# Attention scores from one 128-row matmul on twelve-bit parts in place of four 32-row fp32 tiles

## The chip, the cores and the metric

The kernel runs on one core of a Trainium2 chip. The metric is the device time of one execution in microseconds (us), lower is better; the median of three runs is given. In profiles PE is TensorE, PEld its weight loads, DVE VectorE, ACT ScalarE, POOL GpSimd and SP SyncE, which here only issues DMAs.

## What is computed

The input x has four images of 64 x 64 tokens with 256 channels, all fp32. Two layers follow each other. The first is an attention over the 4096 tokens of an image, with keys f and queries g of 32 channels and values of 128. The second is a triangle attention over the 64 x 64 grid with eight heads, followed by a layer norm, an MLP and another layer norm.

```python
xt = x.reshape(b, hw, c)
f = xt @ Wf + bf
g = xt @ Wg + bg
v = xt @ Wh + bh
s = jnp.einsum('bqd,bkd->bqk', g, f)
beta = jax.nn.softmax(s, axis=-1)
o = jnp.einsum('bqk,bkd->bqd', beta, v)
x = x + (o @ Wo + bo).reshape(b, h, w, c)
...
scores = jnp.einsum('bilhd,bljhd->biljh', q, k) / np.sqrt(d_k)
att = jax.nn.softmax(scores, axis=2)
out = jnp.einsum('biljh,bilhd,bljhd->bijhd', att, v1, v2)
h = _layer_norm(x_in + out.reshape(B, N, N, E) @ Wo, ln_agg_g, ln_agg_b)
return _layer_norm(jax.nn.relu(h @ W1 + b1) @ W2 + b2 + h, ln_out_g, ln_out_b)
```

The change concerns f, g and s.

## The kernel before

`run` goes through the four images ("batches") one after the other. For each there is an attention stage (`layer0`) and then a triangle stage (`first_layer1` for batch 0, `next_layer1` for the others).

**The factors g and f.** `factors` (L236) makes g and f of 512 tokens in one PSUM bank; four blocks of 128 tokens lie on the four groups of 32 partitions. ScalarE adds the biases on the way to a tile `gf` in SBUF (`biased`, L248, instructions of L251). The tile is stored to DRAM, g and f apart, and read back in the layout that the scores need: `spread_g` (L255) puts g of all 4096 tokens on 32 partitions, once for each of four partition groups, as the tile `gT` [128, 4096]; `spread_f` (L261) puts a quarter of f on each group, as `fT` [128, 2, 512]. For batch 0 this is done at the start (`front0`), the stores on ScalarE's queue and the spreads on GpSimd's. For batches 1 to 3 it is done ahead, within batch 0's triangle stage: `Ahead` takes 24 pieces s of 512 tokens each through words of a fixed order, `ORDER0`. Word P transposes the input, C copies it, v and u make the values, g makes the factors, a adds the biases and stores (`factored`, L366, whose tile has one buffer); the digit behind the letter names the piece of the period, and "/2" means two periods late. `Ahead.fetch` (L373) reads what batch b + 1 needs while batch b's triangle stage is in its last steps: g at steps 24 to 27, the first half of v at 28, x at 29 and 30, f after the last piece, the rest at the end, all on SP's queue.

**The attention stage.** `layer0` has eight rows of queries (qb, 512 tokens) times eight groups of keys (k, 512 tokens). `scores(g)` (L522) makes the scores of one group as [keys, queries]: four matmuls, each on its own 32 rows of the array, for four blocks of 128 keys. ScalarE takes the exponential of two PSUM banks at a time (L533), `values(g)` multiplies it with v (L544, four matmuls of 128 rows that add up in one bank), and VectorE sums the exponentials for the denominator (L551). The scores of group g + 1 are issued ahead of the values of group g. `parts` puts the work on the previous row of queries behind the groups: at k = 0 the denominator's matmul (L561), reciprocal (L563) and division (L565), at k = 1 the output matmul (L586), then the projections for the second layer.

**The triangle stage.** 32 steps (NSTEP), each with eight products of attention weights and v2 (`product`, L946), two or three of them on GpSimd and the others on VectorE, and the matmuls that sum them (L956). The order of the words in each period is written out by hand in `ORDER0` and `ORDER`. For batches 1 to 3 the layer norms and the MLP of the batch before run among them (`Tokens`), with some small operations and two passes of 128x512 (`finish`, L1182 and L1183) on GpSimd.

**Buffers.** The large tiles share tags of the pool `big`: "v2" has two buffers of 16 KB a partition (v2 of two head pairs, gT, half of v), "qk" one of 16 KB (q and k, half of v), "S" two. `fT` shares the tag "hid".

**A second run.** `run(safe=True)` repeats all with a maximum taken off the scores, only if the recorded denominators leave a range. It isn't executed on these inputs. It uses bf16 copies of g and f (`reduced`, `max_piece`).

Of the kernel before, what the change touches and what calls it, by code (L numbers as in the profile page):

```python
# [11 lines left out]
BF16 = mybir.dt.bfloat16  # L12
AF = mybir.ActivationFunctionType
# [3 lines left out]
P = 128  # L17
# [3 lines left out]
N = 64  # L21
# [33 lines left out]
    t0/1 v2/2 n1/2 R25/2 A25/2 R33/2 sp0/1 T21/2 A32/2 C30/2 R34/2 R36/2 R30/2 A33/2 e00/1 u2/2 e01/1  # L55
    o1/2 R31/2 g2/2 P00/1 c0/1 R37/2 A34/2 A36/2 A30/2 A31/2 A37/2 V0/1 R35/2 C00/1 T30/2 t1/1 R00/1
    p1/2 P01/1 a2/2 C01/1 A35/2 R03/1 T31/2 A00/1 R02/1 g0/1 a0/1 R05/1 R07/1 A05/1 A03/1 v3/2 R06/1
    u3/2 m0/1 S2/1 W2/1 c1/1 v0/1 V1/1 R01/1 A02/1 n0/1 R04/1 A07/1 A01/1 A04/1 R12/1 P11/1 u0/1 P10/1
    A06/1 T00/1 sp1/1 C11/1 T01/1 R13/1 R15/1 R14/1 A13/1 e10/1 e11/1 t2/1 C10/1 R10/1 A12/1 R17/1 V2/1
    A15/1 A14/1 A10/1 R16/1 R11/1 S0 R22/1 W3/1 g3/2 c2/1 W0 A17/1 R27/1 A11/1 v1/1 R20/1 a3/2 u1/1 o0/1  # L60
    p0/1 S1 R21/1 T10/1 P20/1 t3/1 P21/1 A16/1 T11/1 C20/1 A20/1 R23/1 A22/1 R24/1 R26/1
# [4 lines left out]
def attention_then_triangle_kernel(  # L66
# [144 lines left out]
    class Front:  # L211
        def alloc(self, name):
            if name == "g":
                self.gT = big.tile([P, T], F32, tag="v2", name="gT", bufs=2)
            elif name == "f":
                self.fT = work.tile([P, 2, 512], F32, tag="hid", name="fT", bufs=1)
            elif name == "lo":

                lo = big.tile([P, 4096], F32, tag="qk", name="vlo")
                self.fB = lo[:, 2048:2560].bitcast(BF16).rearrange("p (t k) -> p t k", t=2)  # L220
                self.v = [lo[:, 0:2048].rearrange("p (n d) -> p n d", d=P)]
            elif name == "hi":

                hi = big.tile([P, 4096], F32, tag="v2", name="vhi", bufs=2)
                self.gB = hi[:, 2048:4096].bitcast(BF16)
                self.v.append(hi[:, 0:2048].rearrange("p (n d) -> p n d", d=P))
            else:
                if name == "x0":
                    self.yT = []
                self.yT.append(big.tile([P, T], F32, tag="S", name="yT", bufs=2))  # L230

        def reduced(self):
            for q in range(8):
                nc.gpsimd.tensor_copy(self.gB[:, ts(q, 512)], self.gT[:, ts(q, 512)])
            nc.gpsimd.tensor_copy(self.fB, self.fT)
# [11 lines left out]

    def biased(ps, t):  # L248
        ps = ps.rearrange("p (w t) -> p w t", w=4)
        for w, bias in enumerate((bias_g, bias_f)):  # L250
            nc.scalar.activation(t[:, w, 0:P], ps[:, w, :], AF.Identity, bias=bias)  # L251
# [3 lines left out]
    def spread_g(F, r, d, q0=0, q1=8, queue=nc.sync):  # L255
        queue.dma_start(
            out=F.gT[ts(r, CQK), 512 * q0 : 512 * q1].rearrange("c (q t) -> c q t", t=P),
            in_=d[q0:q1].rearrange("q (n c) t -> c (q n) t", n=4),
        )

    def spread_f(F, q, d, queue=nc.sync):  # L261
        queue.dma_start(
            out=F.fT[ts(q % 4, CQK), q // 4, :].rearrange("c (n t) -> c n t", t=P),
            in_=d[q].rearrange("(n c) t -> c n t", n=4),
        )


    def front0(b):
        F = Front()
        for name in ("x0", "x1", "g", "f", "lo", "hi"):  # L270
            F.alloc(name)
        d = {n: dram.tile([8, P, P], F32, tag="ah" + n, name="ah" + n, bufs=NB) for n in ("g", "f")}
# [18 lines left out]
        for q in range(8):  # L291
            ahead = turned(q + 1) if q < 7 else None
            col = ts(q, 512)
            gf = work.tile([P, 2, C], F32, tag="st", name="gf", bufs=3)
            ps = pb("gf")
            factors(ps, [F.yT[cc][:, col] for cc in range(2)])
            biased(ps, gf)
            for w, n in enumerate(("g", "f")):
                nc.scalar.dma_start(out=d[n][q], in_=gf[:, w, 0:P])
            if ahead:  # L300
                taken(*ahead)
            ps = pc("vp")
            for n in range(4):
                for cc in range(2):
                    nc.tensor.matmul(
                        ps[:, ts(n, P)], F.yT[cc][:, ts(q * 4 + n, P)], wh_sb[:, cc, :],
                        start=(cc == 0), stop=(cc == 1),
                    )
            nc.vector.tensor_copy(
                F.v[q // 4][:, q % 4 * 4 : q % 4 * 4 + 4, :], ps.rearrange("p (n d) -> p n d", n=4)  # L310
            )
            if q % 4 == 3:
                for r in range(4):
                    spread_f(F, q - 3 + r, d["f"], nc.gpsimd)
                    spread_g(F, r, d["g"], q - 3, q + 1, nc.gpsimd)
# [4 lines left out]
    class Ahead:  # L320
        def __init__(self):
            shapes = {"x": [C, T], "v": [P, NKC, P], "g": [8, P, P], "f": [8, P, P]}
            self.d = {
                b: {n: dram.tile(sh, F32, tag="ah" + n, name="ah" + n, bufs=NB) for n, sh in shapes.items()}
                for b in range(1, NB)
            }
            self.n = 8 * (NB - 1)
            self.tp, self.xT, self.vp, self.gf = {}, {}, {}, {}
# [37 lines left out]
        def factored(self, s):  # L366
            t = work.tile([P, 2, C], F32, tag="h", name="gf", bufs=1)
            biased(self.gf.pop(s), t)
            for w, n in enumerate(("g", "f")):
                nc.sync.dma_start(out=self.d[1 + s // 8][n][s % 8], in_=t[:, w, 0:P])  # L370


        def fetch(self, F, b, step):  # L373
# [3 lines left out]
            if 24 <= step < 28:  # L377
                spread_g(F, step - 24, d["g"])
            if step == 28:
                F.alloc("lo")  # L380
                nc.sync.dma_start(out=F.v[0], in_=d["v"][:, 0:16, :])
# [5 lines left out]
            if step == 31:  # L387
                F.alloc("f")
                for q in range(8):
                    spread_f(F, q, d["f"])  # L390
            if step == 32:
                F.alloc("hi")
                nc.sync.dma_start(out=F.v[1], in_=d["v"][:, 16:32, :])
                F.alloc("x1")
                nc.sync.dma_start(out=F.yT[1], in_=d["x"][P : 2 * P, :])
# [70 lines left out]
    def layer0(b, F, safe, rest):  # L466
# [4 lines left out]
        if safe:  # L471
            F.reduced()

# [9 lines left out]
        def max_piece(qc, t, mx):  # L483
            rows = slice(32 * (t % 4), 32 * (t % 4) + 32)
            ps = pb("mxp")
            nc.tensor.matmul(ps, F.gB[rows, ts(qc, P)], F.fB[rows, t // 4, :], start=True, stop=True)
            nc.vector.tensor_reduce(mx[:, qc % 4, t : t + 1], ps, AX.X, ALU.max)
# [28 lines left out]
        def scores(g):  # L516
# [3 lines left out]
            for r in range(4):  # L520
                rows = slice(32 * r, 32 * r + 32)
                nc.tensor.matmul(  # L522
                    s_ps[r // 2][:, r % 2, :], fT[rows, tt, ts(n, P)], gT[rows, ts(qb, QB)],
                    start=True, stop=not safe,
                )
            for r in range(4 if safe else 0):
                one = slice(32 * r, 32 * r + 1)
                nc.tensor.matmul(
                    s_ps[r // 2][:, r % 2, :], ones_b[one, :], row[qb][one, :], start=False, stop=True
                )  # L530
# [115 lines left out]
        def proj_qk(qk, st):  # L646
# [14 lines left out]
            nc.scalar.mul(qk[:, 0, 1792:2048], ps[0][:, 0:256], scale1)  # L661
            nc.scalar.copy(qk[64:128, 1, 1536:2048], ps[1][64:128, :])
# [132 lines left out]
    class Layer1:  # L795
# [10 lines left out]
        def fetch_qk(self, pair, first=False):  # L806
            io, rows = self.io, ts(pair, 64)
            qk = self.qk[pair] = big.tile([P, 2, 2048], F32, tag="qk", name="qk")
            n = 56 if first else 64
            for lh in range(2):  # L810
                half, lk = slice(64 * lh, 64 * lh + 64), min(n - 32 * lh, 32) * N
                nc.sync.dma_start(
                    out=qk[half, 0, 0 : 32 * n], in_=io["q"][rows, lh, 0:n, :].rearrange("c i l -> c (i l)")
                )
                nc.sync.dma_start(out=qk[half, 1, 0:lk], in_=io["k"][rows, 2048 * lh : 2048 * lh + lk])


        def fetch_v2(self, pair, part=None):
            if part != 1:
                self.v2[pair] = big.tile([P, 2, D, N], F32, tag="v2", name="v2", bufs=2)  # L820
# [3 lines left out]
        def fetch_rows(self, pair, l0, l1):  # L824
            v2 = self.v2[pair].rearrange("p h d j -> p (h d j)")
            for i2 in range(2):
                nc.sync.dma_start(
                    out=v2[64 * i2 + l0 : 64 * i2 + l1, :],
                    in_=self.io["v2"][l0:l1, ts(pair, 64), :].rearrange("l c j -> l (c j)"),
                )  # L830


        def scores(self, pair, u):
# [3 lines left out]
            q = qk[:, 0, :].rearrange("p (i l) -> p l i", l=32)  # L837
            k = qk[:, 1, :].rearrange("p (l j) -> p l j", j=N)
# [96 lines left out]
        def product(self, step, m):  # L935
# [10 lines left out]
            eng.tensor_tensor(R, src.unsqueeze(1).to_broadcast([P, D, N]), v2[:, h], ALU.mult)  # L946
# [36 lines left out]
    class Tokens:  # L983
# [6 lines left out]
        def load(self, tt, far=False):  # L990
# [4 lines left out]
            if far:  # L995

                tag = ("v2", "S", "qk")[t % 3]
                both = big.tile([P, 2, 2, 256], F32, tag=tag, name="A", bufs=1 if tag == "qk" else 2)
# [328 lines left out]
    def first_layer1(L, ahead, F):  # L1327
# [10 lines left out]
        def front_word(w, s, cc):  # L1338
            if not 0 <= s < ahead.n:
                return  # L1340
            if w == "P":
                ahead.turned(s, cc)
                turned[s] = turned.get(s, 0) + 1
                if turned[s] == 2:
                    ahead.load(s + 1)
                    if s + 1 == ahead.n:
                        ahead.fetch(F, 1, 31)
# [8 lines left out]
            elif w == "a":  # L1356
                ahead.factored(s)

# [21 lines left out]
    def next_layer1(b, L, rest, ahead, F):  # L1380
# [32 lines left out]
        def of_piece(word, q):  # L1413
# [44 lines left out]
            elif word in ("z0", "z1") and second:  # L1458
# [3 lines left out]
                if F is not None and q == n2 - 1 and ("z", 1 - n) in mps[q]:  # L1462
                    ahead.fetch(F, b + 1, 31)
# [87 lines left out]
```

## Times and profile before

| | us |
|---|---|
| median of 3 runs | 3775.97 |
| lowest and highest run | 3773.95 and 3778.14 |
| span of the profiled execution | 3763.4 |
| TensorE busy in it | 3662.3 |
| VectorE busy | 2623.4 |
| ScalarE busy | 1934.5 |
| GpSimd busy | 1728.9 |

The profiled execution is one execution; its span goes from the first to the last instruction. Its time as a run isn't given apart. The runs' median lies 12.6 us above the span, which is taken as what lies around it. The mean granted clock of TensorE is 0.992.

How to read the parts: busy times are unions, so four matmuls that run side by side on four row groups count once. The page lists two matmul instructions for every fp32 matmul of the program (2048 for the 1024 score matmuls). The groups of the score matmuls, of the values' matmuls and of the two kinds of products, from the list of the costliest groups:

```profile
L946 POOL TENSOR_TENSOR Rp<-attP,v 128x2048 f32<-128x2048 f32 x328 | 1490.3, 4573 | 441.3 <-ACT attP L906 387.5
L946 DVE TENSOR_TENSOR R<-att,v 128x2048 f32<-128x2048 f32 x696 | 1548.1, 2273 | 99.1 <-PE acc L956 59.5
...
L544 PE MATMUL o<-e,vlo 128*128 128x512 f32 x1024 | 475.2, 607 | 0.0
...
L522 PE MATMUL s<-gT,fT 32*128 32x512 f32 x2048 | 300.1, 640 | 3.9 <-ACT e L533 3.7
```

Each line gives line, engine, operation, result and operands, shapes and count; then busy us and the mean ns of one; then the engine's idle time just before them and what ended most of it. The attention stages lie at about 41 to 355, 900 to 1320, 1797 to 2215 and 2698 to 3115 us of the span, the triangle stages between and after them.

### The profile page before, as it was taken

The numbers are of one execution on the slowest core, as the hardware profiler recorded it, in microseconds if no ns is written. First come the engines' busy times: TensorE is split into PE (matmuls) and PEld (weight loads), VectorE is DVE, ScalarE is ACT, GpSimd is POOL, SyncE is SP. The second block draws the span as 40 slices with busy tenths as digits, with TensorE's granted clock in tenths as the row PEclk, the third lists the DMA queues.
The fourth block names the chain that finished last, engine by engine and source line by source line (L and its number), as shares of the span: only waits on it lengthen the run. The fifth ranks groups of instructions, "written<-read, shape, count | busy, mean of one in ns | idle before, by whom it ended". The sixth has DMA issues, their size and how long they took to land.

```text
span 3763.4 us, 60343 instructions
## 1 busy us (share of the span) xinstructions
PE 3662.3 (97%) x23626; PEld 1804.7 (48%) x23626; DVE 2623.4 (70%) x2014; ACT 1934.5 (51%) x4257; POOL 1728.9 (46%) x870
## 2 busy tenths in 40 slices
PE   9999999889999999999999999999999999999998
PEld 5444444444444455554344445555344445555477
DVE  3454499897444469999544449999754445999976
ACT  3333466554333367766333346766533335767654
POOL 4000099895000059999100018999600004999920
PEclk9999999999999999999999999999999999999999
DMA  4111466554111254423111153343211116432221
GB/s 119 46 42 42 113 172 152 147 148 143 45 49 47 74 134 95 93 55 93 57 50 45 53 132 89 76 96 71 93 40 45 53 51 153 93 84 61 67 63 55
DMA packets 446215, 313.65 MB, mean 83 GB/s; under 512 B 299680, under 2 KB 408992, under 8 KB 438624
## 3 DMA queue, kind: packets, MB, share of 16 engines
q1 hardware_dynamic: 427472, 295.84, 29.9%
q10 hardware_dynamic: 15184, 8.06, 0.8%
q0 software_dynamic: 3264, 5.78, 0.7%
q8 instruction: 189, 3.10, 0.4%
q14 instruction: 106, 0.87, 0.1%
HBM read 170.07 MB, written 139.46 MB: 82 GB/s over the span
## 4 chain that ended last, share of the span: by engine, by line
PE 83%; POOL 7%; DMA 3%; issue 2%; DVE 2%; ACT 1%; SPq 0%; ACTq 0%; POOLq 0%; DVEq 0%
PE o L544 25%; PE acc L956 17%; PE proj L601 8%; PE s L522 7%; POOL Rp L946 6%; PE mp L1148 5%; PE zp L1168 5%; PE sp L844 3%; PE hp L1015 2%; PE v1p L633 2%; PE y L586 2%; DVE R L946 1%; DMA qk<-k 1%; PE att L898 1%; PE den L561 1%
## 5 line engine op out<-in xcount | busy, mean ns | idle before, releaser
L946 POOL TENSOR_TENSOR Rp<-attP,v 128x2048 f32<-128x2048 f32 x328 | 1490.3, 4573 | 441.3 <-ACT attP L906 387.5
L946 DVE TENSOR_TENSOR R<-att,v 128x2048 f32<-128x2048 f32 x696 | 1548.1, 2273 | 99.1 <-PE acc L956 59.5
L551 DVE TENSOR_TENSOR esum<-esum,e 128x2048 f32<-128x2048 f32 x224 | 512.7, 2289 | 558.5 <-ACT e L533 555.3
L956 PE MATMUL acc<-R,wsel 128*32 128x512 f32 x5568 | 698.7, 599 | 13.4 <-ACT ao L966 7.5
L533 ACT ACTIVATE e<-s 128x1024 f32<-128x1024 f32 x512 | 496.5, 1021 | 404.1 <-PE s L522 394.7
L1076 POOL TENSOR_SCALAR nt<-mv 128x4 f32<-128x4 f32 (+1 forms) x51 | 9.8, 193 | 1286.9 <-DVE mv L1032 1276.0
L544 PE MATMUL o<-e,vlo 128*128 128x512 f32 x1024 | 475.2, 607 | 0.0
L544 PE MATMUL o<-e,vhi 128*128 128x512 f32 x1024 | 472.8, 605 | 0.0
L956 PE MATMUL acc<-Rp,wsel 128*32 128x512 f32 x2624 | 347.7, 602 | 6.2 <-POOL Rp L946 5.4
L966 ACT COPY ao<-acc 128x1024 f32<-128x1024 f32 x256 | 254.6, 1020 | 178.4 <-PE acc L956 165.9
L956 PEld LDWEIGHTS acc<-R,wsel 128*32 128x32 f32 x5568 | 155.4, 109 | 352.3 <-issue 279.0
L544 PEld LDWEIGHTS o<-e,vlo 128*128 128x128 f32 x1024 | 184.6, 190 | 281.8 <-issue 281.8
L544 PEld LDWEIGHTS o<-e,vhi 128*128 128x128 f32 x1024 | 184.3, 189 | 279.7 <-issue 279.7
L522 PE MATMUL s<-gT,fT 32*128 32x512 f32 x2048 | 300.1, 640 | 3.9 <-ACT e L533 3.7
L881 ACT ACTIVATE es<-S,rd 128x64 f32<-128x64 f32 x1024 | 257.8, 336 | 10.2 <-DVE rd L873 8.7
L563 DVE RECIPROCAL rec<-den 128x512 f32<-128x512 f32 x32 | 107.4, 3357 | 217.3 <-PE den L561 217.3
L1148 PE MATMUL mp<-hT,w 128*128 128x256 f32 x1024 | 249.5, 389 | 0.7 <-ACT hT L1120 0.7
L1168 PE MATMUL zp<-w,hid 128*128 128x256 f32 x1024 | 244.9, 384 | 0.8 <-ACT hid L1157 0.8
L1148 PEld LDWEIGHTS mp<-hT,w 128*128 128x128 f32 x1024 | 186.5, 190 | 101.4 <-ACT attP L906 36.0
L1168 PEld LDWEIGHTS zp<-w,hid 128*128 128x128 f32 x1024 | 185.5, 190 | 63.0 <-issue 30.2
L613 ACT COPY st<-proj 128x512 f32<-128x512 f32 x98 | 57.3, 585 | 288.4 <-PE proj L601 160.3
L854 ACT ACTIVATE S<-sp 128x512 f32<-128x512 f32 x128 | 129.6, 1115 | 91.5 <-PE sp L844 91.5
(177 smaller groups left out, 3701.3 us busy)
## 6 DMA issues: line engine op xcount, KB each, us to landing
v<-v2d SPq DMA_DIRECT2D x22, 1024.0 KB
v1c<-v1d SPq DMA_DIRECT2D x128, 128.0 KB
aT<-ao SPq DMA_DIRECT2D x1024, 16.0 KB
A<-aT SPq DMA_DIRECT2D x256, 64.0 KB
out_dram<-z SPq DMA_DIRECT2D x63, 256.0 KB
y<-yT SPq DMA_DIRECT2D x56, 256.0 KB
q<-st SPq DMA_DIRECT2D x56, 256.0 KB
qk<-k SPq DMA_DIRECT2D x28, 512.0 KB
```

Source lines behind the costliest of these rows:

```text
L522: nc.tensor.matmul(s_ps[r // 2][:, r % 2, :], fT[rows, tt, ts(n, P)], gT[rows, ts(qb, QB)], start=True, stop=not safe,)
L533: nc.scalar.activation(e[g][:, 2 * j : 2 * j + 2, :], s_ps[j], AF.Exp)
L544: nc.tensor.matmul(o_ps[qb], F.v[tt][:, r * 4 + n, :], es[:, r, :], start=(k == 0 and r == 0), stop=(k == 7 and r == 3),)
L551: nc.vector.tensor_tensor(esum[qb], esum[qb], es, ALU.add)
L601: nc.tensor.matmul(ps, w[:, cc, rows], y(qb, cc), start=(cc == 0), stop=(cc == 1))
L854: nc.scalar.activation(self.S[pair][:, :, l0 : l0 + 8].rearrange("p i l -> p l i"), sp[:, lh], AF.Copy if self.safe else AF.Exp,)
L881: nc.scalar.mul(e[:, i, :], rows[:, i, :], rec[:, i : i + 1])
L946: eng.tensor_tensor(R, src.unsqueeze(1).to_broadcast([P, D, N]), v2[:, h], ALU.mult)
L956: nc.tensor.matmul(acc[32 * c : 32 * c + 32, n % 2, :], w[:, n, c, 16 * h : 16 * h + 32], R[:, ts(c, 8), :].rearrange("p d j -> p (d j)"), ...
L966: nc.scalar.copy(self.ao[step][:, ts(np, 2)].rearrange("p k d j -> p k (d j)"), self.acc[step][np])
L1148: nc.tensor.matmul(self.mp[:, fc % 2, :], w1_sb[:, cc, ts(fc, P)], self.hT[tt][:, cc, :], start=(cc == 0), stop=(cc == 1),)
L1168: nc.tensor.matmul(zp[:, n, :], self.hid[tt][:, fc, ts(n, P)], w2_sb[:, fc, :], start=(fc == 0), stop=(fc == 3 and tt not in self.hT2),)
```

## The change

`biased` now writes each of g and f twice: as fp32 into t[:, 1] and, as float32r, into t[:, 0]. [...]t[:, 0] is the upper twelve-bit part. `parted` subtracts it from the full value on VectorE, which leaves the lower part. The tile with both parts of both factors (256 KB) is stored in one DMA on SP's queue. The spreads put the parts on the four row groups so that group r holds part r % 2 of g and part r // 2 of f: one matmul over all 128 rows then adds the four products of parts. The tiles gT and fT are float32r in two halves each, and their DMAs are issued on GpSimd's queue. `scores` makes each block of 128 keys with one such matmul.

For the halves, the large buffers are cut in two: "v2" has four of 8 KB and "qk" two; q and k, the halves of v and of v2 become tiles of their own, and v2 is loaded by four DMAs in place of two. For batches 1 to 3, a new word b (`parted`) stands behind each a in `ORDER0`, f is fetched at step 28 and after the last step in place of after the last piece. The bf16 copies and `reduced` go away.

```diff
+PART = mybir.dt.float32r
...
-    t0/1 v2/2 n1/2 R25/2 A25/2 R33/2 sp0/1 T21/2 A32/2 C30/2 R34/2 R36/2 R30/2 A33/2 e00/1 u2/2 e01/1
+    t0/1 v2/2 n1/2 R25/2 A25/2 R33/2 b1/2 sp0/1 T21/2 A32/2 C30/2 R34/2 R36/2 R30/2 A33/2 e00/1 u2/2 e01/1
...
-    p1/2 P01/1 a2/2 C01/1 A35/2 R03/1 T31/2 A00/1 R02/1 g0/1 a0/1 R05/1 R07/1 A05/1 A03/1 v3/2 R06/1
-    u3/2 m0/1 S2/1 W2/1 c1/1 v0/1 V1/1 R01/1 A02/1 n0/1 R04/1 A07/1 A01/1 A04/1 R12/1 P11/1 u0/1 P10/1
+    p1/2 P01/1 a2/2 C01/1 A35/2 R03/1 T31/2 A00/1 R02/1 b2/2 g0/1 a0/1 R05/1 R07/1 A05/1 A03/1 v3/2 R06/1
+    u3/2 m0/1 S2/1 W2/1 c1/1 v0/1 V1/1 R01/1 b0/1 A02/1 n0/1 R04/1 A07/1 A01/1 A04/1 R12/1 P11/1 u0/1 P10/1
...
-    p0/1 S1 R21/1 T10/1 P20/1 t3/1 P21/1 A16/1 T11/1 C20/1 A20/1 R23/1 A22/1 R24/1 R26/1
+    p0/1 S1 R21/1 T10/1 P20/1 t3/1 P21/1 A16/1 T11/1 C20/1 A20/1 R23/1 b3/2 A22/1 R24/1 R26/1
...
-                self.gT = big.tile([P, T], F32, tag="v2", name="gT", bufs=2)
+                self.gT = [big.tile([P, T // 2], PART, tag="v2", name="gT", bufs=4) for _ in range(2)]
...
         for w, bias in enumerate((bias_g, bias_f)):
-            nc.scalar.activation(t[:, w, 0:P], ps[:, w, :], AF.Identity, bias=bias)
+            nc.scalar.activation(t[:, 1, w, :], ps[:, w, :], AF.Identity, bias=bias)
+            nc.scalar.activation(t[:, 0, w, :].bitcast(PART), ps[:, w, :], AF.Identity, bias=bias)
+
+    def parted(t):
+        nc.vector.tensor_tensor(t[:, 1].bitcast(PART), t[:, 1], t[:, 0], ALU.subtract)
...
+    def store_parts(d, q, t, queue):
+        queue.dma_start(out=d[q], in_=t)
...
+    def spread_g(F, r, d, half):
+        nc.gpsimd.dma_start(
+            out=F.gT[half][ts(r, CQK), :].rearrange("c (q t) -> c q t", t=P),
+            in_=d[4 * half : 4 * half + 4, :, r % 2, 0, :].rearrange("q (n c) t -> c (q n) t", n=4),
         )
...
+    def spread_f(F, r, d, half):
+        nc.gpsimd.dma_start(
+            out=F.fT[half][ts(r, CQK), :].rearrange("c (q t) -> c q t", t=P),
+            in_=d[4 * half : 4 * half + 4, :, r // 2, 1, :].rearrange("q (n c) t -> c (q n) t", n=4),
         )
...
         def factored(self, s):
-            t = work.tile([P, 2, C], F32, tag="h", name="gf", bufs=1)
-            biased(self.gf.pop(s), t)
-            for w, n in enumerate(("g", "f")):
-                nc.sync.dma_start(out=self.d[1 + s // 8][n][s % 8], in_=t[:, w, 0:P])
+            self.t[s] = parts_tile(tag="h", bufs=1)
+            biased(self.gf.pop(s), self.t[s])
+
+        def parted(self, s):
+            t = self.t.pop(s)
+            parted(t)
+            store_parts(self.d[1 + s // 8]["gf"], s % 8, t, nc.sync)
...
             if 24 <= step < 28:
-                spread_g(F, step - 24, d["g"])
+                for half in range(2):
+                    spread_g(F, step - 24, d["gf"], half)
             if step == 28:
                 F.alloc("lo")
+                for r in range(4):
+                    spread_f(F, r, d["gf"], 0)
...
-            if step == 31:
-                F.alloc("f")
-                for q in range(8):
-                    spread_f(F, q, d["f"])
             if step == 32:
                 F.alloc("hi")
+                for r in range(4):
+                    spread_f(F, r, d["gf"], 1)
...
             for r in range(4):
-                rows = slice(32 * r, 32 * r + 32)
                 nc.tensor.matmul(
-                    s_ps[r // 2][:, r % 2, :], fT[rows, tt, ts(n, P)], gT[rows, ts(qb, QB)],
+                    s_ps[r // 2][:, r % 2, :], fT[tt][:, ts(r * 4 + n, P)], gT[qb // 4][:, ts(qb % 4, QB)],
                     start=True, stop=not safe,
                 )
...
-            qk = self.qk[pair] = big.tile([P, 2, 2048], F32, tag="qk", name="qk")
+            qk = self.qk[pair] = [big.tile([P, 2048], F32, tag="qk", name=name, bufs=2) for name in ("q", "k")]
...
-                self.v2[pair] = big.tile([P, 2, D, N], F32, tag="v2", name="v2", bufs=2)
+                self.v2[pair] = [big.tile([P, D, N], F32, tag="v2", name="v2", bufs=4) for _ in range(2)]
...
+            elif w == "b":
+                ahead.parted(s)
```

## The prediction

> **What bounds the kernel now.** I read the page's busy time per engine first, then its chain of waits by engine, then the timeline of a clean stretch of the attention stage, and last the windows and timelines of the triangle stages, to which the change adds work.
>
> ```profile
> PE 3662.3 (97%) x23626; PEld 1804.7 (48%) x23626; DVE 2623.4 (70%) x2014; ACT 1934.5 (51%) x4257; POOL 1728.9 (46%) x870
> ...
> PE 83%; POOL 7%; DMA 3%; issue 2%; DVE 2%; ACT 1%; SPq 0%; ACTq 0%; POOLq 0%; DVEq 0%
> ```
>
> TensorE is the bound over the span, but GpSimd holds 7% of the chain: it is a bound somewhere. The timeline of the attention stage at 60 us shows what one group of scores costs:
>
> ```profile
> 59.65 1.14 PE L522 MATMUL s<-gT,fT 32*128 32x512 f32 x8
> ...
> 60.72 0.30 PEld L544 LDWEIGHTS o<-e,vlo 128*128 128x128 f32 x2 [0.76 <-issue]
> 60.73 3.70 PE L544 MATMUL o<-e,vlo 128*128 128x512 f32 x8
> 60.85 1.94 ACT L533 ACTIVATE e<-s 128x1024 f32<-128x1024 f32 x2 [2.79 <-PE s L522]
> 61.26 0.19 PEld L544 LDWEIGHTS o<-e,vlo 128*128 128x128 f32 x1 [0.24 <-issue]
> ...
> 61.69 0.19 PEld L544 LDWEIGHTS o<-e,vlo 128*128 128x128 f32 x1 [0.24 <-issue]
> ...
> 64.36 1.14 PE L522 MATMUL s<-gT,fT 32*128 32x512 f32 x8
> ```
>
> Groups follow each other every 4.71 us (64.36 less 59.65). The weight loads of the values are 0.43 us apart (61.69 less 61.26), and each fp32 matmul shows as two such instructions, so the four value matmuls stream for 8 x 0.43 = 3.44 us. The remaining 1.27 us is what the four row tiles of scores cost: eight instructions on four row groups, about 2 x 0.43 of streaming, the rest going in and out. ACT works 1.94 of the 4.71 us. So every tenth cut from the score slot shortens the attention stage.
>
> In the triangle stages it is otherwise. The windows of batch 1's last steps, and three that cover batch 0's triangle (columns: window, its length, then busy us of PE, PEld, DVE, ACT, POOL; granted clock, DMA share, GB/s):
>
> ```profile
> 1690.00:1790.00 100.00, 93.68 (x678) 44.21 (x680) 98.68 (x67) 62.53 (x186) 97.41 (x55) 0.99 0.37 95
> ...
> 470.00:650.00 180.00, 174.90 (x1970) 87.37 (x1974) 169.67 (x99) 109.22 (x273) 171.25 (x39) 0.99 0.63 160
> 650.00:790.00 140.00, 126.11 (x1437) 63.61 (x1429) 125.66 (x76) 79.21 (x202) 126.91 (x29) 0.98 0.53 141
> 790.00:895.00 105.00, 93.54 (x984) 46.07 (x984) 96.75 (x52) 52.91 (x139) 98.29 (x22) 0.98 0.61 179
> ```
>
> There PE has 6 to 11% to spare and GpSimd is the busier engine; in batch 0 VectorE, GpSimd and PE are nearly level. And in batch 0 ScalarE waits for the store of the factors (timeline of ACT, then of SP's queue):
>
> ```profile
> 739.27 0.36 ACT L251 ACTIVATE gf<-gf,bias_f 128x128 f32<-128x128 f32 x1
> ...
> 745.27 0.37 ACT L251 ACTIVATE gf<-gf,bias_g 128x128 f32<-128x128 f32 x1 [3.28 <-DMA ahf<-gf]
> ```
>
> ```profile
> 740.97 0.38 SPq L370 DMA_DIRECT2D ahf<-gf  x1
> ...
> 742.01 5.19 SPq L975 DMA_DIRECT2D aT<-ao  x8
> ```
>
> The gf tile has one buffer there, so the next factors can't be written until the last store has landed (4.3 us after its issue).
>
> **What the Trainium skill says.** (1) "FP8 and Floating Point Precision", section TensorE Precision Notes: true FP32 takes four passes, while "FP32 reduced precision" reads four bytes and truncates to FP22. The trace agrees on the first: 4 x 0.215 us. No one-pass matmul of 512 columns is in it. (2) "TensorE: Matmul & The Clock Gate", section Wait — 56ns, not 53.3ns?: 512 columns, warm, 215.7 ns from start to start; half of the 0.43 us above. (3) "TensorEngine Tiling (Array Packing)", section Key Properties: changing the tiling mode drains the engine. The trace agrees in so far as 0.4 us of the slot is not streaming. (4) "DMA: Bandwidth & Descriptors", section SWDGE vs HWDGE vs iDMA: a DMA into float32r counts as a cast, and casts are issued from GpSimd alone. That is why the spreads leave SP's queue; before has no casting DMA.
>
> **The change, part by part.**
>
> Scores. Removed: 256 groups of four 32-row fp32 tiles (1.27 us each). Added: 256 groups of four full-height float32r matmuls of 512 columns. Cost of one: 0.2155 us if it is one pass at full rate, 0.43 if four-byte operands stream at half rate. I take one pass, by (1): 4 x 0.2155 = 0.86 us, with no tiling switch left. Weight loads fit: two in a row take 0.30 us in the lines above, so 0.11 us each in throughput, below 0.2155. A drain between float32r and fp32 isn't shown; bounds 0 to 0.2 us at each end, and I take 0. Gain 0.40 us x 252 groups (the first of each batch waits for ACT) = 101 us. ACT stays within the new 4.3 us. What is late next is the division at the head of each row of queries: the reciprocal (3.36 us) and the product oT end at 194.36, the output matmul starts at 194.78. With 0.40 us less ahead of it the slack is 0.02 us plus a semaphore; 0.1 us x 28 = 3 us given back. Net -98.
>
> Parts. ACT's `biased` goes from two activations to four: two of them start 0.27 us apart, so +0.54 us x 32 = 17 us of ACT, which is 50 to 60% busy; taken at nothing outside of the stall below. VectorE gets `parted`, 32 subtractions of 128x256: 128x1024 takes 1.23 and 128x512 about 0.7 us, so about 0.44 us; 24 fall in batch 0's triangle, 10.6 us on an engine busy 90 to 94%. Half is on the path: +5 (0 to 10.6).
>
> The store's turn. In the order of words b2 stands just ahead of a0, so a0's activations on ACT now wait for VectorE to reach `parted`, for SP to issue one store, and for its landing. Before, the two stores went out right after a2. In the example VectorE ends its run of products at 745.36; plus 0.44 is 745.8; SP is then in the eight aT stores till 747.2; plus 4.3 of landing gives 751.6 against 745.27, +6.3. The same sum at the other two such places (a0 at 799.60 and 853.73) gives 806.6 and 860.5, +7.0 and +6.8. Behind a0 on ACT stand the values' copy, es and attP; GpSimd waits for attP, with about 1 us to spare (749.19 to 750.59). Of 20 us I put 15 on the path (5 to 25).
>
> Spreads on GpSimd. Before: 4 + 8 DMAs a batch on SP, which delay nobody. After, for each of batches 1 to 3: 8 of g at steps 24 to 27, 4 of f at step 28, 4 of f after the last step. Each has the shape of the prologue's gT spread: 0.66 us of GpSimd. With its gap 0.75. The first also waits for VectorE's last product on the old buffer: in batch 1 that ends at about 1690.8, GpSimd's own product ahead of it at 1691.08, so no wait. The four of the end start once GpSimd is done and must land before the fifth group of scores some 15 us later; a landing is 4.5 us: free. Twelve lie among GpSimd's products, where it is busy without a gap: 12 x 0.75 = 9 us a batch, 27 for three. Bounds 0.56 (the smallest such issue) to 1.6 (the longest) each, so 20 to 58. SP loses twelve issues a batch and one of the two stores; its gain is in the sums above.
>
> The rest. Halved qk and v2 tiles double v2's loads on SP, which no engine waits for except as above: nothing, +5 if SP runs late. The prologue's eight later spreads of 256 KB end about 2 us later than now; the last lands near 37 us, scores start at 40.7: nothing. The end of batch 0 has one more store ahead of the last factors: +2.
>
> Sum: -98 + 5 + 15 + 27 + 2 = -49. The profiled execution's span is 3763.4, so 3714. The median of the runs is 3775.97, 12.6 us above that span; what lies around it is kept: 3727.
>
> **The rivals.**
>
> A, as summed, 3727. For it: PE-bound slots, and the reading of (1). Own range: gain 95 to 105, losses 30 to 90: 3701 to 3771.
>
> B, float32r streams at half rate, two passes' time. For it: the fp32 instructions take 0.43 us, which would also fit four bytes read in two cycles. Against: (1) and (2), which know one pass as N columns in N cycles. Slot 1.72, +0.45 x 252 = +113, plus the 49 of losses: 3938.
>
> C, the casting DMAs hold GpSimd. Place: steps 24 to 28 of three batches. Price: 36 issues. Without them the balance is -76, so it decides from 2.1 us an issue. At 3 us: 3776 - 76 + 108 = 3808. For it: no cast is in the trace, and one issue in the prologue took 1.6 us. Against: the bytes and descriptors are the same as the plain spread's.
>
> D, the engine drains between float32r and fp32: 0.2 us lost a group, gain 48 instead of 98: 3777.
>
> That the twelve-bit parts don't hold, so that the guarded second run starts, I give 1%.
>
> **How the numbers follow.** A 0.70, B 0.12, C 0.10, D 0.07, second run 0.01. A measurement here can't tell 0.2% (7.6 us) from no change. Of A 0.02 lies within it, and 0.05 of D; 0.01 of D on either side. Faster 0.69, same 0.07, slower 0.24. The range takes A's own and D, and C as far as 2.8 us an issue: 3697 to 3800; B stays outside.
>
> **What would show it.** Right: score groups of four instructions with some 0.22 us between starts, 4.3 us from group to group, attention stages some 25 us shorter each; in batch 1's and 2's last steps 9 us more, with GpSimd's spreads between its products; three waits of ACT for the store of 9 to 12 us instead of 3 to 6. Wrong: starts 0.43 us apart (B), spreads above 2 us (C), or a gap at each end of the scores (D).

## The result and the profile after

The changed kernel takes 3772.1 us (median of 20 runs, 3767.04 to 3775.47) against 3773.95 us for the kernel before (20 runs beside them). The ratio is 0.9996, interval [0.9989, 1.0002]: no change, where 3727 us was forecast. The profiled executions differ by +6.9 us (spans 3770.3 and 3763.4), the medians by -1.9. In every run whose span is on record the time lies 1.8 to 2.4 us above it, so the 12.6 us given above for the kernel before are no fixed surplus: its profiled execution was some 9 us faster than its median. Up to that much of the losses below is the difference between single executions.

The page's busy time of TensorE and the chain of waits by engine, after:

```profile
PE 3602.1 (96%) x22602; PEld 1943.0 (52%) x22602; DVE 2692.7 (71%) x2046; ACT 1933.0 (51%) x4321; POOL 1762.6 (47%) x918
...
PE 63%; POOL 6%; issue 2%; DVE 1%; DMA 1%; ACT 1%; SPq 0%; ACTq 0%; POOLq 0%
```

TensorE is busy 60 us less and the span is not shorter: the time became waiting elsewhere. The chain's shares add up to only three quarters of this span, so the stages are read one by one. Their lengths in us, each stage from its first score matmul or its first product to the next one's:

| | prologue | attention 0 | triangle 0 | attention 1 | triangle 1 | attention 2 | triangle 2 | attention 3 | triangle 3 and end |
|---|---|---|---|---|---|---|---|---|---|
| before | 40.7 | 425.8 | 433.3 | 450.2 | 447.5 | 452.3 | 448.5 | 452.0 | 613.1 |
| after | 41.9 | 403.5 | 496.5 | 435.9 | 459.1 | 430.6 | 459.2 | 430.6 | 613.0 |
| difference | +1.2 | -22.3 | +63.2 | -14.3 | +11.6 | -21.7 | +10.7 | -21.4 | -0.1 |

The attention stages gave 79.7 us. The triangle stage of batch 0 took back 63.2 of them, those of batches 1 and 2 another 22.3. First the gain, in the timeline of an attention stage of the kernel after:

```profile
61.90 1.48 PE L523 MATMUL s<-gT,fT 128*128 128x512 f32 x4
...
63.22 3.59 PE L544 MATMUL o<-e,v 128*128 128x512 f32 x8
...
66.25 1.48 PE L523 MATMUL s<-gT,fT 128*128 128x512 f32 x4
```

Four score instructions stand in place of eight, and groups follow each other every 4.35 us (66.25 less 61.90) where it was 4.71. Less the 3.44 us of the values' matmuls, a slot of scores is now 0.91 us. The starts of the four lie 0.63, 0.23 and 0.23 us apart (61.90, 62.53, 62.76 and 62.99 in the trace).

Then the loss. The windows of batch 0's whole triangle stage, before and after (length; busy us of PE, PEld, DVE, ACT, POOL):

```profile
sum 433.30, PE 399.73 PEld 200.28 DVE 394.53 ACT 246.66 POOL 399.93; mean PE 399.73 PEld 200.28 DVE 394.53 ACT 246.66 POOL 399.93
```

```profile
sum 496.50, PE 423.40 PEld 211.49 DVE 458.31 ACT 257.72 POOL 411.60; mean PE 423.40 PEld 211.49 DVE 458.31 ACT 257.72 POOL 411.60
```

The stage is 63.2 us longer and VectorE is busy 63.8 us longer; its time without work is 38.8 us before and 38.2 after. The groups of that window show what it is busy with, and what ScalarE waits for:

```profile
L247 DVE TENSOR_TENSOR gf<-gf 128x256 fp32r<-128x256 f32 x23 | 66.2, 2877 | 3.0 <-ACT gf L244 3.0
...
L243 ACT ACTIVATE gf<-gf,bias_g 128x128 f32<-128x128 f32 x23 | 8.4, 366 | 68.9 <-DMA ahgf<-gf 50.3 <-DVE rd L874 9.3 <-PE gf L234 9.2
```

The subtraction of `parted` takes 2.88 us in the mean, not the forecast 0.44. One of them, in the timeline:

```profile
797.79 13.51 POOL L947 TENSOR_TENSOR Rp<-attP,v 128x2048 f32<-128x2048 f32 x3
...
803.10 8.50 DVE L247 TENSOR_TENSOR gf<-gf 128x256 fp32r<-128x256 f32 x1
...
811.25 1.33 POOL L258 DMA_DIRECT2D gT<-ahgf  x2
811.52 0.67 DVE L872 TENSOR_REDUCE dens<-S 128x8 f32<-128x512 f32 x1
811.62 0.33 SPq L253 DMA_DIRECT2D ahgf<-gf  x1
...
814.52 0.37 ACT L243 ACTIVATE gf<-gf,bias_g 128x128 f32<-128x128 f32 x1 [14.71 <-DMA ahgf<-gf]
...
815.69 0.43 DVE L247 TENSOR_TENSOR gf<-gf 128x256 fp32r<-128x256 f32 x1 [1.10 <-ACT gf L244]
815.71 2.42 PEld L354 LDWEIGHTS vp<-wh,xT 128*128 128x128 f32 x11 [9.57 <-ACT gf L244]
```

It starts while GpSimd has three products back to back and ends at 811.60, 0.3 us after the last of them (797.79 + 13.51 = 811.30). The store behind it, the next factors on ScalarE (14.71 us of waiting) and TensorE (9.57 us) all follow. The same instruction at 815.69, after the products, takes 0.43 us.

In batch 1's last steps the windows answer to those shown of before:

```profile
1729.00:1829.00 100.00, 86.41 (x621) 39.62 (x623) 90.97 (x61) 57.89 (x171) 97.36 (x62) 0.99 0.50 89
```

GpSimd is as busy as it was (97.4 us), with the spreads among its work, while VectorE falls from 98.68 to 90.97 us and TensorE from 93.68 to 86.41. TensorE waits 8.7 us for GpSimd's products there, against 1.3 before, and VectorE 7.9 us for TensorE.

### The profile page after: what moved, and what is told of

Read it like the earlier page. It is cut to its first block, busy times and chain, and to the rows that moved or that the text cites. A ratio compares the mean times of both kernels' runs of the same rounds, so it can differ in the third digit from the quotient of the medians.

```text
span 3770.3 us, 58477 instructions
## 1 busy us (share of the span) xinstructions
PE 3602.1 (96%) x22602; PEld 1943.0 (52%) x22602; DVE 2692.7 (71%) x2046; ACT 1933.0 (51%) x4321; POOL 1762.6 (47%) x918
## 4 chain that ended last, share of the span: by engine, by line
PE 63%; POOL 6%; issue 2%; DVE 1%; DMA 1%; ACT 1%; SPq 0%; ACTq 0%; POOLq 0%
PE o L544 17%; PE acc L957 14%; PE proj L601 6%; PE mp L1149 5%; PE zp L1169 5%; POOL Rp L947 5%; PE s L523 5%; PE sp L845 2%; PE hp L1016 2%; PE v1p L633 2%; PE y L586 1%; PE att L899 1%; DMA k<-k 1%; PE htp L1116 1%; PE hp L1021 1%
## 5 line engine op out<-in xcount | busy, mean ns | idle before, releaser
L544 PE MATMUL o<-e,v 128*128 128x512 f32 x2048 | 920.9, 592 | 0.0
L544 PEld LDWEIGHTS o<-e,v 128*128 128x128 f32 x2048 | 388.2, 190 | 392.5 <-issue 370.7
L523 PE MATMUL s<-gT,fT 128*128 128x512 f32 x1024 | 374.8, 487 | 13.1 <-ACT e L533 10.1
L523 PEld LDWEIGHTS s<-gT,fT 128*128 128x128 f32 x1024 | 192.3, 190 | 149.0 <-issue 107.7
L957 PEld LDWEIGHTS acc<-Rp,wsel 128*32 128x32 f32 x2624 | 81.2, 111 | 204.9 <-issue 126.6
```

The source lines that it names most:

```text
L523: nc.tensor.matmul(s_ps[r // 2][:, r % 2, :], fT[tt][:, ts(r * 4 + n, P)], gT[qb // 4][:, ts(qb % 4, QB)], start=True, stop=not safe,)
L544: nc.tensor.matmul(o_ps[qb], F.v[tt][:, r * 4 + n, :], es[:, r, :], start=(k == 0 and r == 0), stop=(k == 7 and r == 3),)
L957: nc.tensor.matmul(acc[32 * c : 32 * c + 32, n % 2, :], w[:, n, c, 16 * h : 16 * h + 32], R[:, ts(c, 8), :].rearrange("p d j -> p (d j)"), ...
```

## The experiments

The theories. 1: the subtraction has two operands in SBUF, and VectorE is held with it while GpSimd works. 2: the store's place behind word b holds ScalarE, since the gf tile has one buffer. 3: the spreads on GpSimd take its time. Diffs are against the changed kernel, except for the two runs with dead instructions. The table has all runs; "stage" is batch 0's triangle stage, and "rest" its length less VectorE's busy time in it.

| run | median us | ratio to before | stage | VectorE busy | rest |
|---|---|---|---|---|---|
| before | 3773.95 | 1 | 433.3 | 394.5 | 38.8 |
| after | 3772.1 | 0.9996 [0.9989, 1.0002] | 496.5 | 458.3 | 38.2 |
| e_zero | 3743.8 | 0.9921 [0.9904, 0.9937] | 469.7 | 394.9 | 74.8 |
| e_pool | 3748.2 | 0.9936 [0.9919, 0.9952] | 469.1 | 395.0 | 74.1 |
| e_psum | 3720.1 | 0.9857 [0.9841, 0.9873] | 449.8 | 406.5 | 43.3 |
| e_sp | 3753.3 | 0.9946 [0.9930, 0.9963] | 492.1 | 445.7 | 46.4 |
| e_early | 3708.4 | 0.9831 [0.9816, 0.9846] | 436.6 | 395.0 | 41.6 |
| e_place | 3774.1 | 1.0006 [0.9997, 1.0014] | 501.2 | 464.6 | 36.6 |
| e_both | 3700.8 | 0.9811 [0.9797, 0.9824] | 449.5 | 406.5 | 43.0 |
| e_junk | 3809.5 | 1.0094 [1.0076, 1.0112] | 474.5 | 437.0 | 37.5 |
| e_junk1 | 3772.1 | 1.0001 [0.9993, 1.0010] | 443.0 | 402.4 | 40.6 |
| e_best | 3772.4 | 1.0004 [0.9996, 1.0012] | 511.2 | 395.8 | 115.4 |

**No subtraction (e_zero).** ScalarE writes the lower part as the bias alone, which is zero in these inputs, so the scores rest on the upper parts; the store stays at word b.

```diff
-            nc.scalar.activation(t[:, 1, w, :], ps[:, w, :], AF.Identity, bias=bias)
+            nc.scalar.activation(t[:, 1, w, :].bitcast(PART), ps[:, w, :], AF.Identity, bias=bias, scale=0.0)
...
-        nc.vector.tensor_tensor(t[:, 1].bitcast(PART), t[:, 1], t[:, 0], ALU.subtract)
+        pass
```

> Leaves out the lower twelve-bit parts: ScalarE writes zeros in their place (scale 0), and word b only stores; VectorE has no subtraction, so the scores come from the upper parts alone. Theory 1 (the subtraction reads two SBUF operands and is blocked while GpSimd runs a product; the 24 subtractions cost VectorE 67 us where 10.6 were counted, and the store behind each is late): batch 0's triangle falls from 496 us to 450-460, the median from 3772 to 3727-3737. Theory 2 (what costs is the place of the store in the queue, behind the aT stores on SP, whatever the subtraction takes): it falls by 10 at most, median 3760 or more. Theory 3 (the spreads on GpSimd): no change but noise. In all of them batches 1 and 2 keep their 459 us.

The stage gets 27 us shorter, less than theory 1 gave (450 to 460 us), and VectorE's busy time is that of before, but the rest doubles to 74.8 us: with the subtraction gone, something else is late.

**Subtraction on GpSimd (e_pool).** `nc.vector` becomes `nc.gpsimd` in `parted`.

> The subtraction of each piece is issued on GpSimd in place of VectorE, at the same place of the order. Theory 1: nothing can block VectorE any more, and GpSimd pays 24 x about 0.7 us = 17 us in batch 0's triangle, some of it in its gaps: that stage 465-475 us, median 3740-3752. Theory 2: the store comes at GpSimd's turn, which is no earlier: 490-505 us, median 3765-3785. Theory 3: worse than the change, as GpSimd has more to do: above 3780.

0.73 us each, and the stage is the same as with none. So for the stage it matters that the subtraction isn't VectorE's, not that it is gone.

**One operand in PSUM (e_psum).** The lower part comes from the PSUM bank with a single SBUF operand, right behind word a, and its store with it; ScalarE's fp32 copies go away.

```diff
-            nc.scalar.activation(t[:, 1, w, :], ps[:, w, :], AF.Identity, bias=bias)
...
+            nc.vector.scalar_tensor_tensor(
+                t[:, 1, w, :].bitcast(PART), ps[:, w, :], bias, t[:, 0, w, :], ALU.add, ALU.subtract
+            )
```

> VectorE makes the lower part from PSUM (bank + bias - upper part, one operand in PSUM and one in SBUF), right behind word a, the store too; ScalarE's second pair of activations is gone. Both theory 1 and theory 2 expect most of batch 0's loss back: the stage 440-455 us, median 3715-3731. If the operands in SBUF were not the reason, the 48 small instructions still show 3 us and more each; by theory 1 they take 0.2-0.35 us each beside GpSimd's products. Theory 3: no gain beyond 10 us.

The two groups in the list of that run, between 440 and 960 us:

```profile
L248 DVE SCALAR_TENSOR_TENSOR gf<-gf,bias_g 128x128 fp32r<-128x128 f32 x24 | 8.2, 343 | 21.3 <-ACT gf L243 21.0
L248 DVE SCALAR_TENSOR_TENSOR gf<-gf,bias_f 128x128 fp32r<-128x128 f32 x24 | 8.2, 341 | 0.0
```

Beside the same products of GpSimd, no one of the 48 takes more than 0.351 us. But operand, place and ScalarE's work changed together here; the next runs part them.

**The spreads on SyncE (e_sp).** Source and destination are viewed as fp32, so that the DMAs of batches 1 to 3 can go through SyncE's queue again.

```diff
-    def spread_g(F, r, d, half):
-        nc.gpsimd.dma_start(
-            out=F.gT[half][ts(r, CQK), :].rearrange("c (q t) -> c q t", t=P),
+    def spread_g(F, r, d, half, queue=nc.sync):
+        queue.dma_start(
+            out=F.gT[half][ts(r, CQK), :].bitcast(F32).rearrange("c (q t) -> c q t", t=P),
```

> The spreads of batches 1 to 3 are issued on SP's queue again, into the same tiles viewed as fp32 (a plain copy of the stored parts); the subtraction stays as in the change. Theory 3 as the whole cause: batches 1 and 2 back to 448 us each and batch 0 to 440-450, median about 3700. Theory 1 with the prediction's price for the spreads (12 x 0.75 us in each of three stages): batches 1 and 2 at 448-450, batch 0's triangle 485-490, median 3742-3752.

The triangle stages of batches 1 and 2 get 8.0 and 7.1 us shorter, that of batch 0 4.4 us. Batch 1's last steps, in the windows of this run, look like before's again (VectorE 98.91, TensorE 92.97):

```profile
1718.00:1818.00 100.00, 92.97 (x680) 43.81 (x676) 98.91 (x67) 61.69 (x184) 97.41 (x55) 1.00 0.39 96
```

**Early store without subtraction (e_early), and with it (e_place).** Subtraction (or none) and place of the store, two by two, with after and e_zero. In both, word a does what word b did; e_early has e_zero's lower part besides.

```diff
         def factored(self, s):
-            self.t[s] = parts_tile(tag="h", bufs=1)
-            biased(self.gf.pop(s), self.t[s])
+            t = self.t[s] = parts_tile(tag="h", bufs=1)
+            biased(self.gf.pop(s), t)
+            parted(t)
+            store_parts(self.d[1 + s // 8]["gf"], s % 8, t, nc.sync)
```

> The lower part is zero, written by ScalarE (no subtraction, as in the run with the zero part), but its store goes out right behind the upper part, at word a, not at word b. Only the store's place differs from the run with the zero part, whose triangle of batch 0 took 469.7 us. Theory 2 (the late store holds ScalarE through the single gf buffer, and this is the part of the loss that the subtraction doesn't explain): 448 to 453 us there, about 3724 us in all. If the place costs no more than the 15 us that was forecast: 455 us or more. If the rest has another cause (four activations, spreads): 468 to 470 us, 3744 us.

> The changed kernel with its subtraction of two SBUF operands kept, but subtraction and store both moved from word b to word a, right behind the activations. Theory 1 (VectorE with two SBUF operands is held while GpSimd works from SBUF): the subtraction still takes 2 to 8 us where GpSimd has products, triangle of batch 0 465 to 485 us against 496.5. If theory 2 alone made the loss, the subtraction's length does not matter once the store is early: 450 to 455 us.

Without the subtraction, the early store is worth 33 us (469.7 to 436.6), more than expected. ScalarE's waits for it, in the view of waits (total us, times, longest), in e_zero and in e_early:

```profile
ACT gf L243 <- DMA ahgf<-gf: 55.1, 7, 12.2
```

```profile
ACT gf L243 <- DMA ahgf<-gf: 19.8, 4, 7.2
```

With the subtraction, the early store is worth nothing: 501.2 us, VectorE busy for 464.6 of them, one subtraction as long as 12.86 us. That is above what either theory gave. The two causes don't add: each alone costs more than 30 us (33.1 for the place; 64.6 for the subtraction with the store early), and both together cost 59.9 over e_early. Where VectorE is held, the store behind it is late from either place, and ScalarE's wait lies within VectorE's.

**Dead instructions in the kernel before: a subtraction of two operands (e_junk), a maximum of one (e_junk1).** These are the direct test of theory 1: 24 more instructions at word a of batch 0 and nothing else, on constant tiles; nobody reads their results.

```diff
+            nc.vector.tensor_tensor(dens[:, 3, 0:256], wq_sb[:, 0, :], wk_sb[:, 0, :], ALU.subtract)
```

```diff
+            nc.vector.tensor_reduce(dens[:, 3, 0:1], wq_sb[:, 0, :], AX.X, ALU.max)
```

> The kernel before with 24 more instructions and nothing else: one VectorE subtraction of 128x256 of two constant SBUF tiles at each word a of batch 0, whose result nobody reads in that time and which waits for no data. Theory 1: where GpSimd has a product in progress it lasts until that ends, 1 to 8 us each, 40 to 70 us in all, and the triangle of batch 0 grows by 10 to 35 us. If the long subtraction of the changed kernel came from a wait for its data or its store: 0.43 us each, 10 us in all, the stage grows by 0 to 10 us.

> The kernel before with 24 more VectorE instructions at the same places as in the run with the dead subtractions, but each reads one SBUF tile of 128x256 (a maximum along the row) in place of two. Theory 1 in its narrow form (only a VectorE instruction with two SBUF operands is held by GpSimd): some 0.35 us each, 8 us in all, and the triangle of batch 0 grows by 6 to 9 us, about 3780 us. If any VectorE instruction that is put there is held by GpSimd, or if the place in the order makes the wait: 1 us or more each, the stage grows by 25 to 41 us as with two operands.

Two operands cost 37.5 us in the medians (by the ratio 0.94%, interval 0.76 to 1.12%, or 29 to 42 us), and 41.2 in the stage of the profiled executions, more than the 10 to 35 expected there. One operand costs 0.4 us (0.01%, -0.07 to 0.10%), where a time of about 3780 us was expected: a miss. Its profiled execution has 9.7 us more in the stage, but it was 5 us slower than its median and that of before 9 us faster, so what the stage gained is open. The 9.5 us of work that it gives VectorE are hardly on the path at all. The listings of the tile `dens` in the two runs (ns minimum, median, maximum; first and last start):

```profile
L369 DVE TENSOR_TENSOR dens<-wq,wk x24: 410/1359/3610, 476.9 to 937.0; 128x256 f32<-128x256 f32 x24
```

```profile
L369 DVE TENSOR_REDUCE dens<-wq x24: 367/406/420, 474.3 to 902.8; 128x1 f32<-128x256 f32 x24
```

The timeline of the run with two operands:

```profile
784.75 4.53 POOL L947 TENSOR_TENSOR Rp<-attP,v 128x2048 f32<-128x2048 f32 x1 [1.27 <-ACT attP L907]
...
786.86 2.71 DVE L369 TENSOR_TENSOR dens<-wq,wk 128x256 f32<-128x256 f32 x1
...
795.59 4.56 POOL L947 TENSOR_TENSOR Rp<-attP,v 128x2048 f32<-128x2048 f32 x1 [1.22 <-PE acc L957]
...
797.70 2.73 DVE L369 TENSOR_TENSOR dens<-wq,wk 128x256 f32<-128x256 f32 x1
```

Each ends 0.28 to 0.29 us after the product beside it (786.86 + 2.71 = 789.57, the product 789.28; 800.43 and 800.15). It is so throughout: of the 72 subtractions of two SBUF operands in after, e_place and e_junk, 54 took more than 0.45 us, and every one of them ends 0.28 to 0.29 us after the end of a product of GpSimd. The 12 that started with no product in progress took 0.41 to 0.43 us. The operands of e_junk have been there since the start, so the wait isn't for data.

The two runs differ also in what is written, 256 elements a partition against one. The products on VectorE itself, listed for the kernel before, speak against the write as the cause:

```profile
L946 DVE TENSOR_TENSOR R<-att,v x696: 2236/2279/2293, 466.5 to 3598.3; 128x2048 f32<-128x2048 f32 x174
```

They write 2048 elements and have one operand in PSUM (att); 692 of the 696 run beside a product of GpSimd, and none takes more than 2.29 us. The Trainium skill has the rule in "SBUF — State Buffer", section Who interferes with whom: a VectorE instruction with two SBUF inputs contends with a GpSimd instruction that reads SBUF, since its second input comes through a read interface that the two share; the lock is exclusive, the order of issue decides who waits, and a `tensor_reduce` on this chip never contends. The three listings agree with it.

**Both gains together (e_both).** e_psum and e_sp in one kernel.

> The one-SBUF-operand lower part with its store right behind the upper part, and the spreads of batches 1 to 3 on SyncE's queue: the two edits that gained alone, together. If their causes are independent, the gains add: 3720 - 52 (VectorE and store) and 3753 - 19 (spreads) give 3772 - 52 - 19 = 3701 us; triangle of batch 0 some 441 us (449.8 less the 9 us of spreads), batches 1 and 2 about 451 us each. If GpSimd's spreads only filled time that the waits of ScalarE left open, the gains overlap and it stays at 3715 to 3720.

3700.8 us: the gains add, and this beats both kernels. The medians gain 19.3 us over e_psum, the profiled executions 16.0: of these 0.3 lie in batch 0's triangle (449.8 and 449.5), 14.7 in those of batches 1 and 2, 3.9 in attention 1, and other stages lose 2.9. The 9 us expected in batch 0 were wrong. That VectorE is the limit there is the likely reason, and the next run put it to the test.

**Subtraction on GpSimd, early (e_best).** Theory 4: in this stage VectorE's busy time plus some 40 us is the length. e_place's edit with `nc.gpsimd` for the subtraction, and e_sp's spreads.

> Subtraction on GpSimd, right behind the activations, with its store there; spreads of batches 1 to 3 on SyncE's queue. Theory 4 (in batch 0's triangle VectorE is the bound: its busy time plus some 40 us is the stage, wherever the store is early): VectorE 395 us busy as before, so 435 to 442 us there against 449.5 in the run that has both edits, and about 3692 us in all. If GpSimd's time counts there as well (413 us busy, some 35 us idle beside it): 448 to 452 us, 3700 to 3705 us.

A miss by 80 us. VectorE's busy time came out as said (395.8 us), the length did not. The timeline of GpSimd at the start of the stage:

```profile
459.04 0.37 ACT L243 ACTIVATE gf<-gf,bias_g 128x128 f32<-128x128 f32 x1 [1.27 <-PE gf L234]
...
460.26 0.73 POOL L247 TENSOR_TENSOR gf<-gf 128x256 fp32r<-128x256 f32 x1 [321.95 <-ACT gf L244]
460.94 13.49 POOL L947 TENSOR_TENSOR Rp<-attP,v 128x2048 f32<-128x2048 f32 x3
```

GpSimd now stands ahead of its first product until ScalarE has come to the factors: 12.5 us of this stage (447.8 to 460.3), and 59 us more over twelve later waits. At word b, as in e_pool, it waits 7.6 us for them in the stage, but the store is late. So theory 4 is no rule: the length follows VectorE's busy time at most while no other engine is made to wait in its queue.

## Why the prediction was wrong

**Scores: right, a size off.** One pass at full rate, not rival B: four instructions in 0.91 us against the forecast 0.86. The gain is 0.36 us a group, not 0.40, and 79.7 us against 98; 5 to 7 of the missing 18 are the late start of attention 1 (below), most of the rest is 0.04 x 252 = 10. The starts within a group lie 0.23 us apart, not 0.2155, which over three or four of them makes the 0.05 us of the slot; why they do was not tried. The 3 us for the reciprocal can't be told apart.

**Parts: the step that failed.** The term was "about 0.44 us", "24 fall in batch 0's triangle", "half is on the path: +5 (0 to 10.6)". The 0.44 us was right for the instruction alone (0.43 in the prologue and at 815.69). But it was read off additions in the attention stage, where GpSimd has no products, and priced into a stage where GpSimd is busy 92% of the time. There it measured 2.88 us, 66.2 us in all. And nearly all of it was on the path: from e_early to e_place VectorE's busy time grows by 69.6 us and the stage by 64.6; in the kernel before, 42.5 us more of it gave 41.2 in the profiled executions and 37.5 in the medians. The bound from above was a bound on the length of the work, not on its wait for a shared resource.

**The store's turn: mechanism right, size too small.** +15 (5 to 25) was forecast; alone it costs 33 us (e_zero to e_early). It adds nothing as long as the subtraction holds VectorE (e_place is no better than after). The forecast summed two terms that overlap.

**Spreads on GpSimd: right.** 0.64 to 0.74 us each, not rival C. 27 us were forecast at 9 a stage; taking them away gave 18.8 us in the medians of after and e_sp (3772.1 less 3753.3), 7 to 8 in each of batches 1 and 2, and 0.3 (e_both) to 4.4 us (e_sp) in batch 0. Of the 22.3 us that these two stages lost, some 15 are the spreads; 4.6 and 2.7 us remain in e_both and were not traced. Two readings of the windows were loose: in the last steps of batch 1 the busiest engine was VectorE (98.68 us), not GpSimd (97.41), and TensorE had 3% to spare, not 6 to 11, in the first 180 us of batch 0's (174.90).

**The rest: +2 forecast, some +5 to +7.** At the end of batch 0 the last factors wait for the store, which stands behind eight aT stores:

```profile
940.12 5.00 SPq L976 DMA_DIRECT2D aT<-ao  x8
...
945.23 0.53 SPq L253 DMA_DIRECT2D ahgf<-gf  x1
...
947.55 0.37 ACT L243 ACTIVATE gf<-gf,bias_g 128x128 f32<-128x128 f32 x1 [5.92 <-DMA ahgf<-gf]
...
949.66 2.13 PE L523 MATMUL s<-gT,fT 128*128 128x512 f32 x4 [6.52 <-ACT e L533]
```

Attention 1 takes 435.9 us where attentions 2 and 3 take 430.6, and where it takes 428.5 itself in e_both.

The sum with what was measured, in the profiled executions: -79.7 for the attention stages (the +5 within them), +59.9 for subtraction and store together, +3.3 for the rest of batch 0's triangle (e_early less before), +22.3 for batches 1 and 2, +1.1 elsewhere: +6.9. The 8.8 us between this and the -1.9 of the medians belong to the fast execution of before and can't be put down to a term. The rival D gave a time near the result (3777) by luck: it needs 0.2 us more for each slot of scores (1.06), and the slot is 0.91.

## What to carry to other kernels

Before an elementwise operation is put on VectorE, look at where its operands lie and at what GpSimd does in that stretch: with both operands in SBUF its price was here the rest of GpSimd's instruction, at times of two or three of them, and the length measured in a stretch without GpSimd said nothing about it. One operand left in PSUM takes the stall away (2.88 us became two times 0.34). A store that frees a single buffer belongs right behind the last write to the tile (worth 33 us here), and two delays in one chain can overlap: here both together cost no more than the longer one, not their sum.

## What the hardware showed beyond the forecast

- A hold can outlast one GpSimd instruction: 8.50 and 12.86 us against products of 4.6 us, where products stood back to back. The dead subtractions were held 3.61 us at most, and one at 759.89 us got in between two products in 0.41 us. Five others of the 72 got in at such a boundary too. What decides this is open.
- In batch 0's triangle the granted clock of TensorE was 0.98 for before and e_early, and 0.93 for after and e_place, which wait more; TensorE was busy 402 us (e_early) and 423 us (after) with the same matmuls. Over all twelve kernels it is the lower the longer the stage, with one swap of neighbours (e_psum and e_both), down to 0.915 at 511 us (e_best), and the dead subtractions alone brought it from 0.98 to 0.94. So the lower clock comes with the waiting and isn't its first cause; how much of the lost time goes through it was not separated.
- A DMA into a tile used as float32r goes through SyncE's queue if the tile is viewed as fp32 (e_sp), and the one that casts on GpSimd takes about as long to issue as the plain one of the prologue did (0.64 to 0.74 us and 0.66).
